# Linear attention block: v's weight applied once per sequence to x^T k, instead of v per tile

## The chip, the cores and the metric

The kernel runs on one core of a Trainium2 chip. The metric is the device time of one execution in microseconds, 2818.39 us as the median of three runs (2816.66 to 2820.75). Engines are called by the names of the profile: PE is TensorE, with PEld its weight loads; DVE is VectorE, ACT is ScalarE, POOL is GpSimd, and SP the engine that issues most of the DMAs.

## The reference, cut to what matters

The input is 16 sequences of 1024 tokens with 512 channels, float32. The block is a linear attention with 16 heads of 32 channels, and then a channel mix; each is added to its input and followed by a layer norm.

```python
qkv = x @ Wqkv.T + bqkv
q, k, v = jnp.split(qkv, 3, axis=-1)
q = rmsnorm(q, gq)
k = rmsnorm(k, gk)
q, k, v = (split(q), split(k), split(v))
q = apply_rope(q, cos, sin)
k = apply_rope(k, cos, sin)
qf = jax.nn.relu(q)
kf = jax.nn.relu(k)
vpad = jnp.concatenate([v, jnp.ones_like(v[..., :1])], axis=-1)
vk = jnp.einsum('bhlp,bhld->bhpd', vpad, kf)
res = jnp.einsum('bhpd,bhld->bhlp', vk, qf)
attn = res[..., :-1] / (res[..., -1:] + EPS_LIN)
attn = attn.transpose(0, 2, 1, 3).reshape(B, L, D)
out = rmsnorm(attn @ Wout.T + bout, gout)
...
x = _layernorm(x + attention(x))
x = _layernorm(x + channel_mix(x))
```

Only vk needs v: per head it is the sum over the sequence's tokens of v times k, and the sum of the keys. Since v = x Wv^T + bv, the sum of v k^T is Wv (sum of x k^T) plus bv times the sum of the keys.

## The kernel before

Tokens are handled in 128 tiles of 128, eight to a sequence. Every float32 product is made of three products of a faster type: hi hi + hi lo + lo hi, where hi is the operand rounded by a copy on ACT and lo the rest, by a subtraction mostly on DVE.

**Part one** (lines 226 to 519) runs `slot(i)` for every tile and three more. A slot loads x of tile i + 2 with channels first (`load_xt`) and the table of tile i + 1 (`tables`: the RMS norm's weight times the rope's cosine and sine; made on POOL for the first eight tiles, L337, stored, and loaded again from then on). On PE it projects q and k (`proj`, L312: 12 matmuls of 512 columns each), then v (12 more), then adds the previous tile's k^T v to four PSUM banks that stand for the whole sequence (`add_kv`, L399 and L407: for each group of four heads a matmul of 258 columns with k's hi and one of 130 with its lo; the columns are v's hi, the keys' scale as hi and lo, and v's lo). On DVE and ACT it adds the bias of q and k (L353), takes the squares (L354), from which POOL takes a power -0.5 (`rsqrt`, L115), multiplies by the two tables (L364, L365), combines them to the rope (L367, L368), splits relu(k) (L373, L374) and scales v (L385, L386, L388, L389); x of the next tile is split (L247, L248). q goes to DRAM through SP (L370). Beside it, `late_weight` splits one chunk of the later weights per slot, the low part on POOL (L258).

At the end of each sequence `finish_a` (one slot after the last add_kv) reads the four banks, masks what doesn't belong to one head, stores the keys' sums and adds v's bias; `finish_b`, a slot later, transposes and splits; `finish_c` multiplies by the output weight in four further slots (L454) and stores the result `m_d`.

Seven tiles (NPRE = 7) begin their second part beside part one, one every eight slots from slot 40 on; the first four go all the way through `part_y` there, the others through `part_q`.

**Part two** (from line 521) takes q, divides by its product with the keys' sums (`part_q`), multiplies by the sequence's matrix (`part_qt`, `part_m`), normalizes (`part_y`), and then runs the channel mix by halves of a sequence (`part_t`, `part_fk`, `part_fr`, `part_fv`), all of whose products are L130. Its pools open as part one's close: `wb` (mixed tokens for the gate, squared keys) right after part one's tiles, `wr` with the gate's weight after slot N has ended the pool of k and v.

The order of the instructions on each engine, SP's DMAs too, is made by the planner of the tile framework from its own estimates of when each becomes ready; each engine then takes its list in order.

Of the kernel before, what the change touches and what calls it, by code (L numbers as in the profile page):

```python
# [17 lines left out]
NC_ = DIM // P  # chunks of 128 channels  # L18
# [3 lines left out]
VW = 2 * P + 2  # v's hi of four heads, the keys' scale as hi and lo, v's lo  # L22
NPRE = 7  # tiles whose second part begins beside the first part
FIRST, STEP = 40, 8  # the first of them, and how many tiles of the first part lie between two
XA = 7  # x tiles in the pool of both parts
XB = 4  # and in the second part's own
HT = 512  # tokens in a half of a sequence
NT = HT // P  # tiles of 128 tokens in a half
# [6 lines left out]
def kernel(  # L35
# [19 lines left out]
    """Post-norm block: relu linear attention with rope, then an RWKV channel mix.  # L55

    x and out are [tiles, 128, 512]; xt is x by tiles with channels first, [tiles, 128, 4, 128]
    (channel = 128 * third + second). Weights are [128, 4, out] with the input channel split the
    same way. Within a head the channels of q and k come even ones first. The rope tables are
    [128, 8, 16] (position = 128 * second + first).  # L60

    A float32 product is three float32r products: hi hi + hi lo + lo hi, with x = hi + lo.
    """
    nc = tc.nc
    V, S, G, T = nc.vector, nc.scalar, nc.gpsimd, nc.tensor
    N = x.shape[0]  # tiles
    NB = N // 8  # sequences
    NH = N // NT  # halves
# [14 lines left out]
    # The second part's own pools, once they are open: x, the sequences' matrices, banks.  # L83
    own = {}

    def ring(tag, n, outer, inner, shape, dtype, name):
        """Slot n of a ring that lies in the pool of both parts and in the second part's own."""
        k = n % (outer + inner)
        pool, size = (wp, outer) if k < outer else (own[tag], inner)
        return pool.tile(shape, dtype, tag=tag, bufs=size, name=name)  # L90
# [17 lines left out]
    # The activation table comes in before the data does.  # L108
# [16 lines left out]
    def product(ps, pairs, rows, cols):  # L125
        """ps = sum over chunks of a^T b, with a and b given as (hi, lo)."""
        n = len(pairs)
        for c, (a, b) in enumerate(pairs):
            for k, (u, w) in enumerate(((0, 0), (0, 1), (1, 0))):
                T.matmul(  # L130
                    ps,
                    lhsT=a[u][:, rows],
                    rhs=b[w][:, cols],
                    start=(c == 0 and k == 0),
                    stop=(c == n - 1 and k == 2),
                )

# [24 lines left out]
    def part_q(j):  # L162
        """relu(q) over its product with the keys' sums."""
# [36 lines left out]
    def layernorm(xt, sm, name):  # L200
        """(x - mean) / sqrt(var + eps), in place; sm holds the sums."""
# [10 lines left out]
    def part_y(j, ps):  # L212
        """Output's bias, its RMS norm, the residual and the layer norm: x becomes x1."""
# [12 lines left out]
    # ================= part one: q, k, v and each sequence's k^T v =================  # L226
    with ExitStack() as a_ctx:
        # What outlives the last tile's projections lies on the other side.
        te = a_ctx.enter_context(tc.tile_pool(name="end", bufs=1, side="right"))
        pa_ctx = a_ctx.enter_context(ExitStack())  # L230
        tk_ctx = a_ctx.enter_context(ExitStack())
        tk = tk_ctx.enter_context(tc.tile_pool(name="endkv", bufs=1, side="right"))
# [18 lines left out]
        w_qkv = {h: ca.tile([P, NC_, 3 * DIM], F32R, name=f"wqkv_{h}") for h in "hl"}  # L251
# [10 lines left out]
        for j in range(3):  # L262
            cols = slice(j * DIM, (j + 1) * DIM)
            for c in range(NC_):
                n = NC_ * j + c
                split_w(
                    w_qkv["h"][:, c, cols],
                    w_qkv["l"][:, c, cols],
# [3 lines left out]
                    *(("x", XA), ("q", 3), ("y", 2))[(n >= XA) + (n >= XA + 3)],  # L272
# [13 lines left out]
        for n, m in (("k", mu_k), ("r", mu_r)):  # L286
# [4 lines left out]
        bvm = te.tile([P, NC_, P], F32, name="bvm")  # L291
        nc.scalar.dma_start(
            out=bvm.rearrange("p g n -> p (g n)"),
            in_=bqkv[2 * DIM : 3 * DIM].partition_broadcast(P),
        )
        # Ones where row and column belong to one head of a group of four.
        mask = te.tile([P, P], F32, name="mask")
# [3 lines left out]
        for g in range(NC_):  # L301
            V.tensor_mul(bvm[:, g, :], bvm[:, g, :], mask)
        state = {}
        ps_kv = {}

        def proj(i, j):
            """A third of the tile's q, k, v."""
            ps = bank(f"ps{'qkv'[j]}{i}")
            cols = slice(j * DIM, (j + 1) * DIM)
            for c in range(NC_):  # L310
                for n, (a, b) in enumerate(((xh, "h"), (xh, "l"), (xl, "h"))):
# [3 lines left out]
                        rhs=w_qkv[b][:, c, cols],  # L315
# [13 lines left out]
        def tables(i):  # L329
            """RMS norm's weight times the rope's cosine and sine, for the positions of tile i."""  # L330
            tab[i] = wa.tile([P, 2, 2 * DIM], F32, tag="tab", bufs=2, name=f"tab{i}")
            t = i % 8
            if i >= 8:
                nc.sync.dma_start(out=tab[i], in_=tab_d[t])
                return
            for n, tb in enumerate((cos, sin)):
                (V if i == 0 and n else G).tensor_mul(  # L337
                    rows(tab[i][:, n, :]),
                    rows(g_qk),
                    tb[:, t, :].unsqueeze(1).to_broadcast([P, 4 * HEADS, HH]),  # L340
                )
            tab_d[t] = dram.tile([P, 2, 2 * DIM], F32, name=f"tab_d{t}")
            nc.sync.dma_start(out=tab_d[t], in_=tab[i])
# [3 lines left out]
        def norm(i, ps):  # L347
            """Bias, and RMS norm's scale (kept apart)."""
            qk = wa.tile([P, 2 * DIM], F32, tag="qk", bufs=2, name=f"qk{i}")
# [8 lines left out]

        def rope(i):
            """RMS norm's weight and the rope; the keys' relu."""  # L360
            qk, tb = qks.pop(i), tab.pop(i)
            t1 = wa.tile([P, 2 * DIM], F32, tag="t1", bufs=1, name=f"t1{i}")
            ro = wa.tile([P, 2 * DIM], F32, tag="ro", bufs=2, name=f"ro{i}")
            V.tensor_mul(t1, qk, tb[:, 0, :])  # L364
            V.tensor_mul(qk, qk, tb[:, 1, :])  # L365
            a1, a2, o = halves(t1), halves(qk), halves(ro)
            V.tensor_sub(o[:, :, 0, :], a1[:, :, 0, :], a2[:, :, 1, :])  # L367
            V.tensor_add(o[:, :, 1, :], a2[:, :, 0, :], a1[:, :, 1, :])  # L368
            q_d[i] = dram.tile([P, DIM], F32, name=f"q_d{i}")
            nc.sync.dma_start(out=q_d[i], in_=ro[:, 0:DIM])  # L370
            kh = tk.tile([P, DIM], F32R, tag="kh", bufs=2, name=f"kh{i}")
            kl = tk.tile([P, DIM], F32R, tag="kl", bufs=2, name=f"kl{i}")
            S.activation(kh, ro[:, DIM : 2 * DIM], AF.Relu)  # L373
            V.scalar_tensor_tensor(  # L374
                kl, ro[:, DIM : 2 * DIM], 0.0, f32(kh), ALU.max, ALU.subtract
            )
            return kh, kl

        def scale_v(i, ps):
            """v times the keys' scale, and the scale itself."""  # L380
            v = tk.tile([P, NC_, VW], F32R, tag="v", bufs=2, name=f"v{i}")
            rs = rstd_all[:, i, 1:2]
            pv = groups(ps)
            vh, vl = v[:, :, 0:P], v[:, :, P + 2 : VW]
            S.activation(vh, pv, AF.Copy, scale=rs)  # L385
            V.scalar_tensor_tensor(vl, pv, rs, f32(vh), ALU.mult, ALU.subtract)  # L386
            rb = rs.unsqueeze(1).to_broadcast([P, NC_, 1])
            V.tensor_copy(v[:, :, P : P + 1], rb)  # L388
            V.tensor_sub(v[:, :, P + 1 : P + 2], rb, f32(v[:, :, P : P + 1]))  # L389
            return v  # L390

        def add_kv(i):
            kh, kl, v = state.pop(i)
            b, t = i // 8, i % 8
            if t == 0:
                ps_kv[b] = pa.tile([P, NC_, DIM], F32, tag="kv", bufs=1, name=f"pskv{b}")
            for g in range(NC_):
                cols = slice(g * P, (g + 1) * P)
                T.matmul(  # L399
                    ps_kv[b][:, g, 0:VW],  # L400
                    lhsT=kh[:, cols],
                    rhs=v[:, g, :],
                    start=(t == 0),
                    stop=False,
                    skip_group_check=True,
                )
                T.matmul(  # L407
                    ps_kv[b][:, g, 0 : P + 2],
                    lhsT=kl[:, cols],
                    rhs=v[:, g, 0 : P + 2],  # L410
                    start=False,
                    stop=(t == 7),
                    skip_group_check=True,
                )

        fin = {}

        def finish_a(b):
            """Block diagonal k^T v (with v's bias) by groups of four heads; the keys' sums."""
            ps = ps_kv.pop(b)  # L420
            kc = te.tile([P, NC_], F32, tag="kc", name=f"kc{b}")
            V.reduce_sum(kc, ps[:, :, P : P + 2], AX.X)
            kv = te.tile([P, NC_, P], F32, tag="kv", name=f"kv{b}")
            S.copy(kv, ps[:, :, P + 2 : VW])
            V.tensor_add(kv, kv, ps[:, :, 0:P])
# [352 lines left out]
```

## Time and profile before

| what | value |
|---|---|
| median of three runs | 2818.39 us |
| profiled execution, span | 2818.5 us |
| instructions | 39315 |
| granted PE clock, mean over the span | 0.994 |
| a tile's DVE work in part one | L364 1.22, L365 1.23, L353 twice 0.69, L248, L367, L368, L374 0.69 each, L386 0.74 us |
| a tile's ACT work in part one | L354 twice 0.63, L247 0.62, L373 0.63, L385 0.69 us |
| POOL in part one, from tile 8 on | L115, 1.65 us a tile |
| loads of a table (1 MB) | 120, 5.2 us from issue to landing |

The profile names a group of instructions by its line, engine and operation, with what it writes and reads. A duration on PE is from issue to the modelled end, and matmuls overlap: how often a new one starts is what counts. The clock of PE granted in the first 100 us is below one, and full after that. DVE's and POOL's durations contain what an instruction waited for inside itself, after it was issued.

### The profile page before, as it was taken

The page shows a single profiled execution, that of the slowest core. Times are in us where ns is not written, and L with a number is a line of the kernel's source. Part 1 is how long each engine was busy: PE and PEld are TensorE (multiplying, and loading weights), DVE is VectorE, ACT ScalarE, POOL GpSimd, SP SyncE. Part 2 cuts the span into 40 slices and gives each one's busy share as a digit, 9 for nine tenths or more (in the row PEclk, how much of TensorE's full clock was granted, in tenths as well). Part 3 has the DMA queues.
Part 4 walks back from the last instruction along what each step waited for, and adds up shares of the span by engine and source line. Part 5 has one row for each costly group of instructions (what it writes and reads, how often), then busy time and mean ns, then how long its engine had stood idle before and what let it go on. Part 6 is the DMA issues. An engine that isn't in the chain of part 4 may idle for free.

```text
span 2818.5 us, 39315 instructions
## 1 busy us (share of the span) xinstructions
PE 2769.1 (98%) x13072; PEld 2295.8 (81%) x13072; DVE 2278.0 (81%) x4999; ACT 1608.8 (57%) x3199; POOL 859.8 (31%) x823
## 2 busy tenths in 40 slices
PE   7899999999999999998999999999999999999998
PEld 5788888888888888887788888888888888888887
DVE  7998888888888888887878788877888787878774
ACT  3343334444333333435677767777777777777775
POOL 7431111111111111113433333333333333333331
PEclk9999999999999999999999999999999999999999
DMA  7566666665656556556132313231323132323210
GB/s 248 190 240 207 189 209 202 192 191 188 202 197 194 207 197 199 187 178 218 64 106 92 111 61 109 87 116 57 113 85 107 64 112 87 101 72 100 81 53 34
DMA packets 165146, 397.78 MB, mean 141 GB/s; under 512 B 24272, under 2 KB 24528, under 8 KB 148560
## 3 DMA queue, kind: packets, MB, share of 16 engines
q1 hardware_dynamic: 162784, 391.74, 42.7%
q10 hardware_dynamic: 2160, 3.54, 0.4%
q8 instruction: 103, 1.69, 0.2%
q14 instruction: 99, 0.81, 0.1%
HBM read 279.84 MB, written 115.38 MB: 140 GB/s over the span
## 4 chain that ended last, share of the span: by engine, by line
PE 50%; DVE 1%; issue 0%; ACT 0%; POOLq 0%; POOL 0%; ACTq 0%
PE psv L130 12%; PE psk L130 12%; PE psr L130 12%; PE psy L130 11%; PE pst L538 2%; PE psqt L181 2%; DVE gate L653 0%; DVE mrl L559 0%; DVE x L655 0%; ACT x L210 0%; DVE mixr L548 0%; DVE pr L166 0%; DVE mixk L548 0%; DVE nmf L209 0%; ACT junkf L205 0%
## 5 line engine op out<-in xcount | busy, mean ns | idle before, releaser
L115 POOL TENSOR_TENSOR rstd_all<-ss,mhalf 128x2 f32<-128x2 f32 x128 | 208.8, 1631 | 911.9 <-DVE ss L355 911.7
L354 ACT ACTIVATE junk<-qk 128x512 bf16<-128x512 f32 x256 | 161.6, 631 | 387.2 <-DVE qk L353 386.4
L130 PE MATMUL psk<-mkh,w_k 128*128 128x512 f32 x1024 | 333.0, 397 | 0.0
L130 PE MATMUL psv<-w_v,kah 128*128 128x512 f32 x1024 | 326.5, 400 | 0.0
L130 PE MATMUL psr<-w_r,mrh 128*128 128x512 f32 x1024 | 323.2, 397 | 0.0
L130 PE MATMUL psy<-mb,qth 128*128 128x512 f32 x1024 | 319.5, 393 | 2.0 <-ACT qth L184 2.0
L221 POOL TENSOR_TENSOR y<-y,g_out 128x512 f32<-128x512 f32 x128 | 168.9, 1319 | 327.8 <-ACT junky L217 326.1
L559 POOL TENSOR_TENSOR mkl<-mixk,mkh 128x512 fp32r<-128x512 f32 x128 | 175.6, 1373 | 182.8 <-ACT mkh L558 182.8
L130 PEld LDWEIGHTS psy<-mb,qth 128*128 128x128 f32 x1024 | 191.8, 188 | 44.7 <-ACT qth L184 2.3
L130 PEld LDWEIGHTS psk<-mkh,w_k 128*128 128x128 f32 x1024 | 193.1, 189 | 39.2
L130 PEld LDWEIGHTS psv<-w_v,kah 128*128 128x128 f32 x1024 | 188.1, 188 | 40.4
L130 PEld LDWEIGHTS psr<-w_r,mrh 128*128 128x128 f32 x1024 | 188.3, 189 | 36.5
L312 PE MATMUL psq<-wqkv_h,xh 128*128 128x512 f32 x512 | 205.4, 401 | 11.6 <-ACT wqkv_h L257 6.4
L312 PE MATMUL psq<-wqkv_l,xh 128*128 128x512 f32 x512 | 203.7, 398 | 0.2 <-POOL wqkv_l L258 0.2
L312 PE MATMUL psq<-wqkv_h,xl 128*128 128x512 f32 x512 | 202.8, 396 | 0.8 <-DVE xl L248 0.8
L130 PE MATMUL psv<-w_v,kal 128*128 128x512 f32 x512 | 202.1, 395 | 0.0
L312 PE MATMUL psv<-wqkv_h,xh 128*128 128x512 f32 x512 | 200.3, 391 | 1.7 <-DVE qk L353 1.2
L312 PE MATMUL psk<-wqkv_h,xh 128*128 128x512 f32 x512 | 200.0, 391 | 2.0 <-DVE v L386 1.8
L130 PE MATMUL psy<-mb,qtl 128*128 128x512 f32 x512 | 201.5, 393 | 0.0
L312 PE MATMUL psv<-wqkv_l,xh 128*128 128x512 f32 x512 | 200.3, 391 | 0.9 <-POOL wqkv_l L258 0.9
L130 PE MATMUL psr<-w_r,mrl 128*128 128x512 f32 x512 | 200.9, 392 | 0.0
L312 PE MATMUL psv<-wqkv_h,xl 128*128 128x512 f32 x512 | 200.8, 392 | 0.0
(135 smaller groups left out, 7252.4 us busy)
## 6 DMA issues: line engine op xcount, KB each, us to landing
tab<-tab_d SPq DMA_DIRECT2D x120, 1024.0 KB, 5.2
xt<-in_xt_dram SPq DMA_DIRECT2D x128, 256.0 KB, 4.8
q_d<-ro SPq DMA_DIRECT2D x128, 256.0 KB, 4.6
m_d<-m SPq DMA_DIRECT2D x64, 512.0 KB, 4.1
mb<-m_d SPq DMA_DIRECT2D x64, 512.0 KB, 7.0
q<-q_d SPq DMA_DIRECT2D x128, 256.0 KB, 2.6
x<-in_x_dram SPq DMA_DIRECT2D x128, 256.0 KB, 2.8
out_dram<-x SPq DMA_DIRECT2D x128, 256.0 KB, 3.0
```

The lines of the kernel that those rows point to most:

```text
L115: G.tensor_tensor(dst, src, mhalf[:, 0 : src.shape[1]], ALU.pow)
L130: T.matmul(ps, lhsT=a[u][:, rows], rhs=b[w][:, cols], start=(c == 0 and k == 0), stop=(c == n - 1 and k == 2),)
L181: T.transpose(ps[:, c, :], q[:, c * P : (c + 1) * P], ident)
L221: G.tensor_mul(y, y, g_out)
L312: T.matmul(ps, lhsT=a[i][:, c, :], rhs=w_qkv[b][:, c, cols], start=(c == 0 and n == 0), stop=(c == NC_ - 1 and n == 2),)
L354: S.activation(junk(f"{i}{j}"), qk[:, cols], AF.Square, accum_out=ss[:, j : j + 1])
L538: T.transpose(ps[:, t * P : (t + 1) * P], xs[NT * s + t][:, c * P : (c + 1) * P], ident)
L559: (V if n == "r" and s != 1 else G).tensor_sub(ml, m, f32(mh))
```

## The change

v is not computed per tile any more. The tile's x is loaded a second time with tokens first, split into hi and lo (`split_xn`: hi on ACT, lo on POOL), and `add_kx` accumulates x^T k over the sequence in four PSUM banks: 12 matmuls of 512 columns per tile. ACT multiplies k by its scale in the relu, and the keys of a sequence are added up on POOL in `acc`. Once per sequence, `finish_a` takes x^T k out of PSUM as hi and lo, `finish_s` sums `acc` over the tokens with a matmul by ones, and `finish_b` multiplies by v's weight (`w_a`), adds v's bias times the keys' sums, masks on POOL and splits. `finish_c` is as it was. v's weight leaves the weights split ahead of the first tile and comes first among the late ones.

The table is now two tiles with one buffer each instead of one with two, `qk` has one buffer instead of two, the rope's first product is written into `ro`, NPRE is 6 instead of 7, and the x tiles are 6 + 5 instead of 7 + 4. `tables(i + 1)` stands at the end of a slot instead of its beginning; `finish_c` stands ahead of `add_kx`. At the handover, slots N + 1 and N + 2 come ahead of the pools `wb` and `wr` and of the load of the gate's weight.

```diff
-NPRE = 7  # tiles whose second part begins beside the first part
+NPRE = 6
-XA = 7  # x tiles in the pool of both parts
-XB = 4  # and in the second part's own
+XA = 6
+XB = 5
...
+        def split_xn(i):
+            w = wa.tile([P, DIM], F32, tag="xn", bufs=1, name=f"xn{i}")
+            nc.sync.dma_start(out=w, in_=x[i])
+            h = tk.tile([P, DIM], F32R, tag="xnh", bufs=2, name=f"xnh{i}")
+            l = tk.tile([P, DIM], F32R, tag="xnl", bufs=2, name=f"xnl{i}")
+            S.copy(h, w)
+            G.tensor_sub(l, w, f32(h))
+            xn[i] = h, l
...
-        for j in range(3):
+        for j in range(2):
...
-        for g in range(NC_):
-            V.tensor_mul(bvm[:, g, :], bvm[:, g, :], mask)
...
+            tab[i] = [
+                wa.tile([P, 2 * DIM], F32, tag=f"tab{n}", bufs=1, name=f"tab{n}{i}")
+                for n in range(2)
+            ]
...
-            qk = wa.tile([P, 2 * DIM], F32, tag="qk", bufs=2, name=f"qk{i}")
+            qk = wa.tile([P, 2 * DIM], F32, tag="qk", bufs=1, name=f"qk{i}")
...
         def rope(i):
-            V.tensor_mul(t1, qk, tb[:, 0, :])
-            V.tensor_mul(qk, qk, tb[:, 1, :])
-            a1, a2, o = halves(t1), halves(qk), halves(ro)
-            V.tensor_sub(o[:, :, 0, :], a1[:, :, 0, :], a2[:, :, 1, :])
-            V.tensor_add(o[:, :, 1, :], a2[:, :, 0, :], a1[:, :, 1, :])
+            V.tensor_mul(ro, qk, tb[0])
+            V.tensor_mul(qk, qk, tb[1])
+            a2, o = halves(qk), halves(ro)
+            V.tensor_sub(o[:, :, 0, :], o[:, :, 0, :], a2[:, :, 1, :])
+            V.tensor_add(o[:, :, 1, :], a2[:, :, 0, :], o[:, :, 1, :])
...
-            S.activation(kh, ro[:, DIM : 2 * DIM], AF.Relu)
-            V.scalar_tensor_tensor(
-                kl, ro[:, DIM : 2 * DIM], 0.0, f32(kh), ALU.max, ALU.subtract
-            )
-            return kh, kl
+            S.activation(k, k, AF.Relu, scale=rstd_all[:, i, 1:2])
+            S.copy(kh, k)
+            V.tensor_sub(kl, k, f32(kh))
+            b, t = divmod(i, 8)
+            ros[i] = k
+            if t == 1:
+                acc[b] = tx.tile([P, DIM], F32, tag="acc", name=f"acc{b}")
+                G.tensor_add(acc[b], ros[i - 1], k)
+            if t > 1:
+                G.tensor_add(acc[b], acc[b], k)
+            return kh, kl
...
+        def add_kx(i):
+            kh, kl = state.pop(i)
+            h, l = xn.pop(i)
...
+            for c in range(NC_):
+                cols = slice(c * P, (c + 1) * P)
+                for n, (a, r) in enumerate(((h, kh), (h, kl), (l, kh))):
+                    T.matmul(
+                        ps_kx[b][c],
+                        lhsT=a[:, cols],
+                        rhs=r,
+                        start=(t == 0 and n == 0),
+                        stop=(t == 7 and n == 2),
+                    )
...
+        def finish_a(b):
+            kx = tx.tile([P, NC_, NC_, 2, P], F32R, tag="kx", name=f"kx{b}")
+            for c, ps in enumerate(ps_kx.pop(b)):
+                S.copy(kx[:, c, :, 0, :], groups(ps))
+                V.tensor_sub(kx[:, c, :, 1, :], groups(ps), f32(kx[:, c, :, 0, :]))
+            fin[b] = kx
+
+        def finish_s(b):
+            a = acc.pop(b)
+            m = te.tile([P, 2, DIM], F32R, tag="m", bufs=2, name=f"ma{b}")
+            S.copy(m[:, 0, :], a)
+            G.tensor_sub(m[:, 1, :], a, f32(m[:, 0, :]))
+            ps = bank(f"psks{b}")
+            for n in range(2):
+                T.matmul(ps, lhsT=ones, rhs=m[:, n, :], start=(n == 0), stop=(n == 1))
+            ksv[b] = tx.tile([P, DIM], F32, tag="ksv", name=f"ksv{b}")
+            S.copy(ksv[b], ps)
...
+        def finish_b(b):
+            kx, ks = fin.pop(b), ksv.pop(b)
...
+            for g in range(NC_):
+                cols = slice(g * P, (g + 1) * P)
+                ps = bank(f"pskv{b}{g}")
+                for c in range(NC_):
+                    T.matmul(
+                        ps[:, 0 : 2 * P],
+                        lhsT=w_a["h"][:, c, cols],
+                        rhs=kx[:, c, g, :, :].rearrange("p two n -> p (two n)"),
...
+                    T.matmul(
+                        ps[:, 0:P],
+                        lhsT=w_a["l"][:, c, cols],
+                        rhs=kx[:, c, g, 0, :],
...
+                kv = te.tile([P, P], F32, tag="kv", bufs=1, name=f"kv{b}{g}")
+                V.scalar_tensor_tensor(
+                    kv, ks[:, cols], bv[:, g : g + 1], ps[:, 0:P], ALU.mult, ALU.add
+                )
+                V.tensor_add(kv, kv, ps[:, P : 2 * P])
+                G.tensor_mul(kv, kv, mask)
+                S.copy(th[:, g, :], kv)
+                G.tensor_sub(tl[:, g, :], kv, f32(th[:, g, :]))
...
-        late = [("o", wout, c) for c in range(NC_)]
+        late = [("a", wqkv[:, :, 2 * DIM : 3 * DIM], c) for c in range(NC_)]
+        late += [("o", wout, c) for c in range(NC_)]
...
         tk_ctx.close()
+        slot(N + 1)
+        slot(N + 2)
+        tx_ctx.close()
+        wb = ctx.enter_context(tc.tile_pool(name="workb", reuse_waits="tile", bufs=1))
         wr = ctx.enter_context(tc.tile_pool(name="workr", reuse_waits="tile", bufs=1))
         load_w("r", wr)
-        slot(N + 1)
         pa_ctx.close()
-        slot(N + 2)
```

## The prediction

> **What bounds the kernel now.** I read the page's busy table and its forty slices first, then the windows by stage, then the groups of lines inside one undisturbed sequence, and last the timeline of the first tiles.
>
> The page, busy time and slices:
>
> ```profile
> PE 2769.1 (98%) x13072; PEld 2295.8 (81%) x13072; DVE 2278.0 (81%) x4999; ACT 1608.8 (57%) x3199; POOL 859.8 (31%) x823
> ...
> PE   7899999999999999998999999999999999999998
> PEld 5788888888888888887788888888888888888887
> DVE  7998888888888888887878788877888787878774
> ACT  3343334444333333435677767777777777777775
> POOL 7431111111111111113433333333333333333331
> ```
>
> TensorE is full except at the start and in slices 18 and 19, where part one hands over. VectorE is next, eight tenths full. GpSimd is busy in the first two slices, nearly empty through part one, and busier again in part two.
>
> Windows (length, then busy time of each engine, granted clock, DMA share, GB/s):
>
> ```profile
> 46.50:112.30 65.80, 56.48 (x234) 45.65 (x234) 63.99 (x73) 19.96 (x42) 44.92 (x20) 0.88 0.63 228
> 112.30:1270.80 1158.50, 1157.09 (x5585) 973.09 (x5584) 960.78 (x1695) 461.94 (x961) 215.00 (x138) 1.00 0.61 198
> 1270.80:1450.00 179.20, 166.00 (x779) 135.36 (x778) 146.99 (x342) 120.58 (x236) 78.33 (x81) 0.97 0.42 135
> ...
> 332.00:408.30 76.30, 76.30 (x370) 64.22 (x369) 62.31 (x109) 30.01 (x62) 13.20 (x8) 1.00 0.60 193
> ```
>
> The first is six slots (tiles 1 to 7): VectorE is full (63.99 of 65.80), TensorE is not. The second is slots 7 to 127, where TensorE has no gap. The third is the handover, 13.2 us of TensorE idle. The last is one sequence, eight slots: 76.3 us, TensorE 76.3, VectorE 62.3, ScalarE 30.0, GpSimd 13.2. So in steady state TensorE sets the time and VectorE has 14 us of slack per sequence.
>
> Groups inside that sequence:
>
> ```profile
> L399 PE MATMUL pskv<-v,kh 128*128 128x258 f32 x32 | 7.9, 319 | 0.0
> L407 PE MATMUL pskv<-v,kl 128*128 128x130 f32 x32 | 7.3, 227 | 0.0
> L440 PE MATMUL pskvt<-ident,kv 128*128 128x128 f32 x4 | 0.6, 272 | 0.0
> L353 DVE TENSOR_TENSOR qk<-psk,b_qk 128x512 f32<-128x512 f32 x8 | 5.5, 692 | 9.7 <-PE psk L312 9.6
> L386 DVE SCALAR_TENSOR_TENSOR v<-psv,rstd_all,v 128x512 fp32r<-128x512 f32 x8 | 6.0, 744 | 0.0
> ```
>
> The matmul rows overlap, so I price TensorE from start to start in the timeline: twelve psv matmuls run from 802.36 to 805.09, 0.227 each; the eight of add_kv from 805.09 to 805.97, 0.88 a slot, 0.22 for a pair of 258 and 130 columns.
>
> The first tiles, VectorE and then GpSimd (start, duration):
>
> ```profile
> 96.24 0.68 DVE L367 TENSOR_TENSOR ro<-t,qk 128x512 f32<-128x512 f32 x1
> 96.84 2.88 DVE L368 TENSOR_TENSOR ro<-qk,t 128x512 f32<-128x512 f32 x1
> 99.65 2.30 DVE L388 CAST v<-rstd_all 128x4 fp32r<-128x4 f32 x1
> 101.99 0.17 DVE L389 TENSOR_TENSOR v<-rstd_all,v 128x4 fp32r<-128x4 f32 x1
> 102.07 0.68 DVE L353 TENSOR_TENSOR qk<-psq,b_qk 128x512 f32<-128x512 f32 x1
> ```
>
> ```profile
> 96.23 2.94 POOL L337 TENSOR_TENSOR tab<-g_qk,cos 128x1024 f32<-128x1024 f32 x1
> 99.14 2.78 POOL L337 TENSOR_TENSOR tab<-g_qk,sin 128x1024 f32<-128x1024 f32 x1
> ```
>
> L368 takes 0.685 in the steady state; here it ends half a microsecond after the GpSimd multiply beside it (99.17). The cast after it waits out the next multiply. VectorE and GpSimd take turns. Operations with a PSUM input are spared: L353 and L386 keep 0.68 and 0.74 in this window. That is the view that decides this case.
>
> **TensorE.** Per slot v's twelve matmuls go and twelve of x^T k come, both 512 wide: 12 x 0.227 each way, nothing. add_kv goes: 8 x 0.88 = 7.0 a sequence, and four transposes, 4 x 0.11 = 0.4. Added per sequence: two 512-wide matmuls for the keys' sum, 0.45, and 16 pairs of 256 and 128 columns at 0.22, 3.5. Net 7.4 - 4.0 = 3.5 us a sequence, so 76.3 becomes 72.8. Over the fifteen sequences of the second window: -52 if TensorE stays the bound.
>
> **VectorE.** Per sequence, out: L386 8 x 0.744, and L388 and L389 8 x (0.172 + 0.162), together 8.6; finish_a and finish_b lose a reduce 0.16, an add 0.68, a multiply 0.69, four L431 at 0.347 and one L444 0.68, 3.6. In: four subtractions from PSUM at 0.685, 2.7; four L431-like and four 128-wide adds, the latter between 0.16 (L389) and 0.347, I take 0.28: 2.5. Splitting the keys stays one operation of 0.68. 62.3 - 8.6 - 3.6 + 2.7 + 2.5 = 55.4.
>
> **GpSimd.** Alone, a two-input 128x512 operation takes 1.29 (L221 in part one), a power 0.55 (two or one columns, from the rows with none of VectorE's work beside them; the 1.65 of L115 is mostly a wait for L365). Per sequence: eight xnl 10.3, seven sums of keys 9.0, one split of the sum 1.3, eight powers 4.4, and eight 128-wide operations of finish_b between 0.55 and 1.29, I take 0.55: 4.4. Together 29.4, against 13.2 busy now.
>
> **What that costs VectorE.** In the 65.8 us window its instructions' durations add up to 69.5; at their undisturbed durations they would be 47.6. So 21.9 were lost. GpSimd's work there, at its undisturbed lengths, is ten table multiplies at 2.37, four splits at 1.29 and six powers at 0.55: 32.2. The ratio is 0.68: each microsecond of GpSimd took 0.68 from a full VectorE. Bounds for the new mix: 0 if every GpSimd operation falls into VectorE's idle time or beside an operation that reads PSUM, 1 if none does. I take 0.68: 0.68 x 29.4 = 20.0, and VectorE needs 55.4 + 20.0 = 75.4 a sequence. That is more than TensorE's 72.8: **VectorE, blocked by GpSimd, becomes the bound, about where TensorE was.**
>
> [...]
>
> The tiles of part two that begin in part one now cost VectorE instead of TensorE: six part_q at 2.76 (L166 to L173), four times part_qt and part_y at some 2.6 plus 1.6 of blocking: 33.5 in all. Steady state: 15 x 75.4 + 33.5 = 1164.5 against 1158.5, **+6**. One hundredth of the ratio is 4.4 us, so break-even for the whole kernel is near 0.64.
>
> **The first tiles.** Six slots at 10.97. VectorE loses 1.08 a slot; GpSimd gains an xnl and a sum, 2.58, and is charged 0.68 of it, 1.75, plus more of the weight splits, which are one a slot for twenty slots instead of sixteen: I take +1.6 a slot, +10, and 4 x 1.29 x 0.68 = 3.5 for the four chunks of v's weight that now come late. Ahead of them: four fewer weight chunks before the first slot, and the four multiplications of v's bias by the mask are gone (7.34 us from 38.62 on, each blocked). I take -6, between -10 and 0. Sum **+7**.
>
> **The handover.** finish_b of the last sequence has 3.5 us more of matmuls and, with one buffer for kv, four rounds VectorE, GpSimd, ScalarE, GpSimd of 0.35 + 0.28 + 0.55 + 0.35 + 0.55 = 2.1 us instead of one wait of 1.83. The pool of part two's gate mix and squared keys now opens only after it, and so do four 512 KB loads of the gate's weight (13.5 us to land). Cover: three early tiles, transposes, four key products of 2.7 us that need only banks. If that cover is short, up to 20; I take **+6**, from -3 to +20.
>
> **At nothing.** x is read once more, 256 KB a slot on SP: DMA share 0.60, by bytes about 0.69. ScalarE rises from 30 to some 37 of 76. A table half is now loaded into its only buffer: freed at the end of its multiply, it lands 5.2 us later and is needed a slot of 9.4 us less 1.2 after that. Its cover is 1.6 to 3 us; see the last rival. Part two's steady state is untouched.
>
> **Sum.** 2818.5 (the profiled span; the median of the runs is 2818.4, the same) + 6 + 7 + 6 = 2837.5, say **2838**.
>
> **Rivals.** (1) TensorE stays the bound: the GpSimd operations fall beside q's and k's bias additions (16 a sequence, spared) and into VectorE's 9.7 us of waits for psk. For it: 17 us of room a sequence below 72.8, and a ratio under 0.59 is enough. Against it: the room is only there as long as VectorE is not late. 2818.5 - 52 + 7 + 6 = **2779**. (2) kv's single buffer stops VectorE: between two groups of finish_b it waits for a GpSimd multiply, a ScalarE copy and a GpSimd subtraction, 1.45 us, four times in sixteen sequences: +93, **2931**. It decides once VectorE has no slack and the order puts nothing between the groups; behind the waiting instruction stand q's and k's bias additions, and behind them the banks. The order is made by a planner that I can't see, hence half of it is as likely: 2885. (3) The tables come late, with q's store ahead of them on SP: 1.8 us in 120 slots, about 3030.
>
> **Chances.** Forecast (2815 to 2870): 0.42. TensorE bound: 0.33. kv's buffer, whole or in part: 0.21. Tables: 0.04. Less than 0.2% (5.6 us, what this kernel's measurement can't tell from nothing) takes 0.08, most of it from the forecast's lower end. Faster 0.34, same 0.08, slower 0.58. The forecast's own range is 2815 to 2870; for 8 in 10, 2774 to 2912.
>
> **What would show it.** After: VectorE 9 in the slices of part one and TensorE below, waits of TensorE there on VectorE; L367-, L368-like and key-split rows well over 0.69, the bias additions not; GpSimd near 30 us a sequence or more; about 75 to 76 us from sequence to sequence. If TensorE has no gap in part one and a sequence takes 73, the first rival holds; if VectorE idles on GpSimd or ScalarE in finish_b, the second. I am wrong altogether if the bias additions are blocked as well, or nothing is.

## The result, and the profile after

The changed kernel takes 2853.59 us (median of four runs, 2852.93 to 2854.51) against 2817.52 before: a ratio of 1.0125, 95% interval 1.0111 to 1.0139. It is 36 us slower; 20 were forecast. The profiled execution spans 2851.2 us, 32.7 more than before.

The page after, busy time and slices:

```profile
PE 2753.0 (97%) x12528; PEld 2251.1 (79%) x12528; DVE 2309.2 (81%) x4674; ACT 1698.0 (60%) x3455; POOL 1288.0 (45%) x1209
...
PE   6899998999999999998999999999999999999998
PEld 5677876777887878886788888888888888888887
DVE  8888888888888888887787878787878787878774
...
POOL 8765544554555555554533333333333333333341
PEclk9899999999999999998999999999999999999999
```

TensorE has 16 us less busy time and a longer span. Between tiles 7 and 127 GpSimd has gone from 19% to 52% of the time. VectorE is not at 9 there, as I had said it would be; it went from 83% to 84%.

The windows after (length, busy time of each engine, granted clock, DMA share, GB/s): the first tiles, tiles 7 to 127, the handover, then a sequence that carries a tile's second part, and a quiet one:

```profile
46.50:108.00 61.50, 50.14 (x186) 38.91 (x185) 58.74 (x47) 19.30 (x44) 57.94 (x28) 0.86 0.45 167
108.00:1293.00 1185.00, 1138.23 (x5064) 927.48 (x5063) 997.04 (x1388) 545.13 (x1205) 618.76 (x506) 0.98 0.69 224
1293.00:1480.00 187.00, 171.16 (x781) 138.59 (x780) 145.18 (x342) 124.23 (x241) 83.46 (x90) 0.94 0.39 132
...
423.00:513.10 90.10, 81.03 (x349) 64.90 (x348) 72.65 (x107) 38.05 (x84) 39.99 (x35) 0.94 0.67 226
1143.20:1218.80 75.60, 74.02 (x331) 61.02 (x330) 64.30 (x89) 35.31 (x78) 38.74 (x32) 0.98 0.68 222
```

Between tiles 7 and 127, TensorE now idles 47 us (1.4 before), and its granted clock is 0.98 instead of 1.00. The quiet sequence takes 75.6 us, 0.2 from my number, but VectorE is busy for 64.3 of them and not for all.

From the start of the first table multiplication of tiles 7, 39, 71 and 127, the time falls into five stages. Sequences are counted from tile 7, eight tiles each; the first two carry late weights, the fifth to eighth a tile's second part each; the last column is from tile 127's multiplication to the end of the span.

| us | to tile 7 | seq. 1 to 4 | 5 to 8 | 9 to 15 | to the end |
|---|---|---|---|---|---|
| before | 112.3 | 304.9 | 322.1 | 531.6 | 1547.7 |
| after | 108.0 | 315.0 | 342.0 | 527.8 | 1558.3 |
| change | -4.3 | +10.1 | +19.9 | -3.8 | +10.6 |
| e1, no wide GpSimd work | 104.6 | 297.6 | 319.1 | 509.8 | 1556.9 |
| e2, it is on VectorE | 108.9 | 303.5 | 317.1 | 512.3 | 1556.1 |
| e3, four kv | 108.3 | 310.9 | 345.0 | 514.4 | 1552.3 |
| e4, scale on x | 109.7 | 309.8 | 333.1 | 519.9 | 1557.3 |
| e5, e2 and e3 | 108.7 | 302.0 | 314.6 | 510.9 | 1555.6 |
| e9, and late weights spread | 109.0 | 299.4 | 312.1 | 510.8 | 1551.8 |

So the loss is 30 us in the first eight sequences, in six of which GpSimd and VectorE have something more to do (called loaded below), and 11 in the handover; the seven quiet ones gain only 4, where TensorE's saved work, 3.2 us each (76.3 before against the 73.1 that e1 and e3 reach below), would give 22.

VectorE's groups in the quiet sequence (busy, mean ns, then idle time before them and what ended it):

```profile
L384 DVE TENSOR_TENSOR ro<-qk,tab 128x1024 f32<-128x1024 f32 x8 | 12.6, 1573 | 0.1
L396 DVE TENSOR_TENSOR kl<-ro,kh 128x512 fp32r<-128x512 f32 x8 | 8.2, 1024 | 9.0 <-ACT kh L395 9.0
L249 DVE TENSOR_TENSOR xl<-xt,xh 128x512 fp32r<-128x512 f32 x9 | 7.7, 853 | 0.0
L388 DVE TENSOR_TENSOR ro<-qk,ro 128x512 f32<-128x512 f32 x8 | 6.6, 822 | 0.0
L372 DVE TENSOR_TENSOR qk<-psq,b_qk 128x512 f32<-128x512 f32 x8 | 5.5, 689 | 0.6
L372 DVE TENSOR_TENSOR qk<-psk,b_qk 128x512 f32<-128x512 f32 x8 | 5.5, 684 | 0.0
L477 DVE SCALAR_TENSOR_TENSOR kv<-ksv,bv,pskv 128x128 f32<-128x128 f32 x4 | 1.4, 340 | 1.3 <-POOL kvtl L483 1.3
```

Four operations with two inputs in SBUF are drawn out beside GpSimd: the first multiplication from 1.22 to 1.57, the split of the keys from 0.68 to 1.02, that of x from 0.69 to 0.85, the last step of the rope from 0.69 to 0.82; together 8 us. The bias additions, which read PSUM, are not (0.69 and 0.68). And there is an idle time that I hadn't priced: 9.0 us in which VectorE stands before the split of the keys until ScalarE has made their high half. For TensorE it doesn't wait in this sequence.

What TensorE waits for in that sequence shows in the timeline at finish_b, TensorE and then VectorE (start, duration, wait in brackets):

```profile
1165.32 0.33 PE L460 MATMUL pskv<-kx,wa_h 128*128 128x256 f32 x1
...
1165.55 0.34 PE L460 MATMUL pskv<-kx,wa_h 128*128 128x256 f32 x1
1165.72 0.22 PE L468 MATMUL pskv<-kx,wa_l 128*128 128x128 f32 x1
1167.34 0.39 PE L460 MATMUL pskv<-kx,wa_h 128*128 128x256 f32 x1 [1.39 <-DVE qk L372]
...
1169.27 0.52 PE L460 MATMUL pskv<-kx,wa_h 128*128 128x256 f32 x1
1169.59 0.31 PE L468 MATMUL pskv<-kx,wa_l 128*128 128x128 f32 x1
1169.69 0.52 PE L460 MATMUL pskv<-kx,wa_h 128*128 128x256 f32 x1
```

```profile
1166.60 0.68 DVE L372 TENSOR_TENSOR qk<-psq,b_qk 128x512 f32<-128x512 f32 x1
1167.20 0.68 DVE L372 TENSOR_TENSOR qk<-psk,b_qk 128x512 f32<-128x512 f32 x1
```

finish_b asks for four banks of a ring of four. The next of them still holds q's projection, which VectorE reads only at 1166.60. TensorE stands for 1.39 us. Less than a microsecond after the gap, at 1168.18, the granted clock falls to half, for 3.41 us: a pair of matmuls takes 0.42 (1169.27 to 1169.69) instead of 0.23 (1165.32 to 1165.55). But that isn't what makes a quiet sequence longer than 73.1 us: sequences 11 to 13, with a wait of 1.1 to 1.4 us at the same place and a granted clock of 1.00 throughout, take 75.6 or 75.7 us as well.

### The profile page after: what moved, and what is told of

The parts are those of the page before. It is cut to its first block, busy times and chain, and to the rows that moved or that the text cites. A ratio compares the mean times of both kernels' runs of the same rounds, so it can differ in the third digit from the quotient of the medians.

```text
span 2851.2 us, 39461 instructions
## 1 busy us (share of the span) xinstructions
PE 2753.0 (97%) x12528; PEld 2251.1 (79%) x12528; DVE 2309.2 (81%) x4674; ACT 1698.0 (60%) x3455; POOL 1288.0 (45%) x1209
## 4 chain that ended last, share of the span: by engine, by line
PE 52%; DVE 1%; ACT 1%; issue 0%; POOL 0%; POOLq 0%; ACTq 0%
PE psk L129 12%; PE psr L129 12%; PE psv L129 12%; PE psy L129 12%; PE psqt L180 2%; PE pst L579 2%; DVE x L222 0%; DVE pr L165 0%; PE pskx L419 0%; DVE mixr L593 0%; DVE mixr L589 0%; DVE y L214 0%; ACT junka L204 0%; ACT x L209 0%; PE psm L493 0%
## 5 line engine op out<-in xcount | busy, mean ns | idle before, releaser
L392 ACT ACTIVATE ro<-ro,rstd_all 128x512 f32<-128x512 f32 x128 | 92.7, 724 | 430.2 <-POOL rstd_all L114 270.2
L327 PE MATMUL psq<-wqk_h,xh 128*128 128x512 f32 x512 | 207.3, 405 | 30.9 <-DVE qk L372 12.4
L261 POOL TENSOR_TENSOR xnl<-xn,xnh 128x512 fp32r<-128x512 f32 x128 | 183.7, 1435 | 96.3 <-ACT xnh L260 93.2
L396 DVE TENSOR_TENSOR kl<-ro,kh 128x512 fp32r<-128x512 f32 x128 | 130.3, 1018 | 106.5 <-ACT kh L395 106.5
L419 PE MATMUL pskx<-kl,xnh 128*128 128x512 f32 x512 | 208.2, 407 | 6.1 <-DVE kl L396 6.1
L419 PE MATMUL pskx<-kh,xnl 128*128 128x512 f32 x512 | 206.8, 404 | 0.0
L327 PE MATMUL psq<-wqk_h,xl 128*128 128x512 f32 x512 | 205.6, 401 | 0.8 <-DVE xl L249 0.8
L327 PE MATMUL psq<-wqk_l,xh 128*128 128x512 f32 x512 | 205.6, 402 | 0.0
L327 PE MATMUL psk<-wqk_h,xh 128*128 128x512 f32 x512 | 201.6, 394 | 3.5 <-DVE qk L372 1.7
L114 POOL TENSOR_TENSOR rsa<-sqa,mhalf 128x1 f32<-128x1 f32 x128 | 81.0, 633 | 268.1 <-DVE sqa L205 200.8
```

The costliest lines, as they stand in the source:

```text
L114: G.tensor_tensor(dst, src, mhalf[:, 0 : src.shape[1]], ALU.pow)
L261: G.tensor_sub(l, w, f32(h))
L327: T.matmul(ps, lhsT=a[i][:, c, :], rhs=w_qk[b][:, c, cols], start=(c == 0 and n == 0), stop=(c == NC_ - 1 and n == 2),)
L392: S.activation(k, k, AF.Relu, scale=rstd_all[:, i, 1:2])
L396: V.tensor_sub(kl, k, f32(kh))
L419: T.matmul(ps_kx[b][c], lhsT=a[:, cols], rhs=r, start=(t == 0 and n == 0), stop=(t == 7 and n == 2),)
```

## The experiments

All are changes of the changed kernel unless said otherwise, and all ratios are to the kernel before, whose median was 2817 to 2818 us beside them.

**e1: no wide GpSimd work.**

```diff
+            if i == 0:
+                xn_l.append(tk.tile([P, DIM], F32R, tag="xnl", bufs=1, name="xnl"))
+                G.tensor_sub(xn_l[0], w, f32(h))
+            xn[i] = h, xn_l[0]
...
-            if t > 1:
-                G.tensor_add(acc[b], acc[b], k)
```

> Leaves out two things: the low half of x is made for tile 0 alone and used for every tile, and only the first two tiles of a sequence are added up in the keys' sum; so GpSimd loses 14 of its 16 wide operations per sequence (18 us) and no other engine gets work. Theory A (GpSimd's wide operations block VectorE, and that is where the time goes): the sequences in part one fall from 75.6 us to TensorE's 72.8, those with late weights and with second parts from 80 to 90 by about as much again, and the whole to 2775 to 2795. Rival B (one buffer for qk, for a table and for kv, and the chain power, scaled relu, copy, split of the keys): those stay as they are, the sequences stay at 75 and the whole above 2835.

2788.34 us, ratio 0.9893 (0.9873 to 0.9913). The quiet sequences take 73.1 us and TensorE is without a gap in them; sequences 1 to 4 lose 17 us, 5 to 8 lose 23. As theory A had it. The handover stays (1556.9), so GpSimd's work per tile has no part in that. The run takes away the work; it doesn't tell whether the drawing out of VectorE's instructions beside GpSimd's (8 us in the changed kernel's quiet sequence) or the lateness of what GpSimd delivers is the cause.

**e2: the same work on VectorE.**

```diff
-            G.tensor_sub(l, w, f32(h))
+            V.tensor_sub(l, w, f32(h))
...
-                G.tensor_add(acc[b], acc[b], k)
+                V.tensor_add(acc[b], acc[b], k)
```

> The low half of x and the sum of the keys are made on VectorE instead of GpSimd. Theory A: VectorE gets 16 x 0.69 = 11 us a sequence of its own and loses the waits of 20.6 us of GpSimd work; at the ratio of 0.31 that the changed kernel shows in its quiet sequences this is a loss of 4 us a sequence, at my 0.68 a gain of 3; so 2830 to 2880, with the first sequences, where GpSimd is full of tables and weights, gaining most. Rival B: VectorE waits for the keys anyway, 9 us a sequence, so the 11 us are half hidden: 2855 to 2900.

2800.66 us, ratio 0.9938 (0.9923 to 0.9953): faster than before, and outside both expectations on the good side. Windows of a sequence with a second part and of a quiet one:

```profile
412.40:497.90 85.50, 81.30 (x360) 66.36 (x359) 74.20 (x123) 39.72 (x86) 19.49 (x20) 0.96 0.73 243
1096.30:1169.40 73.10, 73.10 (x336) 60.36 (x335) 67.52 (x104) 35.83 (x79) 19.27 (x17) 1.00 0.71 230
```

VectorE does 15 more wide operations in the quiet sequence, some 10 us, and is busy for only 3.2 us more than in the kernel with them on GpSimd (67.5 against 64.3). There GpSimd had cost it some 8 us of drawn out instructions, and 9 of waits for the keys stood beside them (1.2 here). Its first multiplication is at 1.25 us again in the loaded sequence (1.46 there with GpSimd).

**e3: four kv.** kv of all four groups lies in one buffer of the ring m.

```diff
+            kvs = te.tile([P, 2 * NC_, P], F32, tag="m", bufs=2, name=f"kvs{b}")
...
-                kv = te.tile([P, P], F32, tag="kv", bufs=1, name=f"kv{b}{g}")
+                kv = kvs[:, g, :]
```

> kv of all four groups lies in one buffer of the m ring instead of one group after the other in a single buffer. Rival B, in the form of my second rival: VectorE no longer waits for GpSimd in finish_b (1.3 us a sequence in the quiet ones) and TensorE no longer for the banks (1.7 us a sequence): 2815 to 2835. Theory A: the waits were in slack, and the result is within 6 us of 2851.

2829.24 us, ratio 1.0033 (1.0019 to 1.0047); 24 us under the changed kernel, as the rival had it. Its windows, a loaded and a quiet sequence:

```profile
419.20:509.10 89.90, 82.72 (x367) 66.69 (x366) 73.33 (x108) 38.07 (x84) 40.73 (x35) 0.96 0.68 226
1132.70:1205.80 73.10, 73.10 (x336) 60.42 (x335) 61.03 (x89) 36.38 (x79) 41.05 (x32) 1.00 0.72 230
```

With GpSimd as busy as after (41.05 us), the quiet sequence is down to 73.1 and TensorE has no gap; no bank is missing at finish_b. The planner's order changed there too, so the run doesn't tell the buffer itself from the order that it allows. The loaded one stays at 90. And the handover loses 6 us. So there are two losses: one at the end of each sequence, which either e2 or e3 takes away, and one in the loaded sequences, which e2 takes away and e3 doesn't.

**e4: the keys' scale on x.**

```diff
-            S.copy(h, w)
-            G.tensor_sub(l, w, f32(h))
+            rs = rstd_all[:, i, 1:2]
+            S.activation(h, w, AF.Copy, scale=rs)
+            V.scalar_tensor_tensor(l, w, rs, f32(h), ALU.mult, ALU.subtract)
...
-            S.copy(kh, k)
-            V.tensor_sub(kl, k, f32(kh))
+            S.activation(kh, k, AF.Relu)
+            V.scalar_tensor_tensor(kl, k, 0.0, f32(kh), ALU.max, ALU.subtract)
+            S.activation(k, k, AF.Relu, scale=rstd_all[:, i, 1:2])
```

> The keys' scale goes to x with tokens first (a scaled copy on ScalarE, the low half on VectorE with the scale) instead of the keys, whose high half is then one relu straight from the rope; the scaled relu for the keys' sum follows off the path. VectorE's split of the keys waits for one ScalarE operation instead of two and no longer for the power. Theory A: it loses 8 GpSimd operations a sequence as e2 does in part, with 5.5 us more on VectorE: 2835 to 2860. Rival B (the chain is what holds VectorE, 9 us a sequence): VectorE's waits for the keys fall below 3 us a sequence, sequences reach 73, and the whole is 2800 to 2825.

2830.84 us, ratio 1.0044 (1.0029 to 1.0059). VectorE's waits for the keys' high half fall from 99.3 us in part one to 5.6, as rival B had it; but the quiet sequences are at 74.1, not 73, and the time lies between the two expectations, 4 us under theory A's and 6 over rival B's. The run takes half of the wide work off GpSimd as well and can't tell which of the two gave its 23 us; e10, beside e5, tries the chain alone.

**e5 and e6: with four kv, both on VectorE, or x's low half alone.** e5 is e2 and e3; e6 leaves the keys' sum on GpSimd.

> e2 and e3 together: the low half of x and the keys' sum on VectorE, and four buffers for kv. Theory A2 (two separate losses: kv's single buffer at the end of each sequence and at the handover, and GpSimd's wide operations where VectorE is full, in the sequences with tables, late weights and second parts): the sequences keep e2's times, and the handover falls by e3's 4 to 6 us: 2787 to 2797. If VectorE, at 70 of 73 us, is now the bound itself, kv's buffer doesn't matter or the order gets worse: 2798 to 2815.

> As e5, but only the low half of x goes to VectorE; the keys' sum stays on GpSimd. Theory A2: half of GpSimd's wide work stays, so the loaded sequences lie between e3's and e2's and the quiet ones at 73.1: 2800 to 2815. If it is the number of VectorE's own operations that costs in the loaded sequences, this beats e5: below 2790.

e5: 2793.0 us, ratio 0.9912 (0.9898 to 0.9925). e6: 2804.13 us, ratio 0.9948 (0.9935 to 0.9962). Both times are as theory A2 says, but not all of its parts: e5's handover is 1555.6, as e2's 1556.1, and not 4 to 6 us less; what e5 gains over e2 lies in the sequences. Beside e5, e6's seven GpSimd additions a sequence cost 11 us, 10 of them in sequences 5 to 8 (324.5 against 314.6).

**e7 and e8: GpSimd work put into the kernel before.** e8 is the kernel before with NPRE 6 and x tiles 6 + 5, e7 has two GpSimd subtractions per tile on top, whose result nobody reads.

```diff
+            for _ in range(2 if i < N else 0):
+                G.tensor_sub(
+                    extra,
+                    xh[i].rearrange("p c n -> p (c n)").bitcast(F32),
+                    xl[i].rearrange("p c n -> p (c n)").bitcast(F32),
+                )
```

> The kernel before with NPRE 6 and x tiles 6 + 5, and two GpSimd subtractions of 128x512 per tile (x's high and low half, of which nothing is used): 20.6 us of GpSimd work a sequence and nothing else. By my ratio 0.68 VectorE is blocked for 14 us a sequence, just its slack of 14: quiet sequences stay at 76.3 to 78, the first tiles take 1.8 us a tile more, those with second parts some 5 us a sequence more; 2840 to 2875. By the ratio 0.31 of the changed kernel the quiet sequences stay at 76.3 exactly and the whole is 2825 to 2845. If GpSimd's work doesn't matter, as e8.

> The kernel before with NPRE 6 and x tiles 6 + 5 alone, the control of e7: one tile less begins in part one, which moves some 3 us of work behind it and takes little cover from the handover: 2812 to 2826.

e8: 2824.32 us, ratio 1.0027 (1.0018 to 1.0037). e7: 2949.52 us, ratio 1.047 (1.0456 to 1.0484): 125 us for 256 unused GpSimd operations, more than twice what I expected at most. A quiet sequence takes 82.6 instead of 76.3. VectorE's groups in one of them, and GpSimd's:

```profile
L369 DVE TENSOR_TENSOR ro<-qk,t 128x512 f32<-128x512 f32 x8 | 14.3, 1782 | 0.0
L390 DVE TENSOR_TENSOR v<-rstd_all,v 128x4 fp32r<-128x4 f32 x8 | 9.3, 1165 | 0.0
L387 DVE SCALAR_TENSOR_TENSOR v<-psv,rstd_all,v 128x512 fp32r<-128x512 f32 x8 | 5.9, 739 | 0.0
L389 DVE CAST v<-rstd_all 128x4 fp32r<-128x4 f32 x8 | 1.4, 171 | 4.1 <-POOL rstd_all L115 4.1
```

```profile
L490 POOL TENSOR_TENSOR extra<-xh,xl 128x512 f32<-128x512 f32 x16 | 25.9, 1621 | 7.7 <-DVE xl L248 6.9 <-DVE v L389 0.2
```

One operation of 0.69 takes 1.78 and a tiny one of 0.16 takes 1.17, each behind one of the two subtractions; L387, which reads PSUM and comes as the second ends, stays at 0.74. That is 8 x (1.10 + 1.00) = 16.8 us of VectorE for 16 x 1.29 = 20.6 us of GpSimd, a ratio of 0.81. VectorE is full (78.3 busy and 4.1 of wait for the power, of 82.6), and TensorE, 79.2 busy, waits for it. Nothing reads what these subtractions make, and the wait for the power is 4.1 in a sequence of the kernel before as well; so this shows by itself what VectorE loses beside GpSimd.

**e9: late weights spread.** e5, with part two's weights split one every third tile after tile 8.

```diff
-            if 1 <= i and late and i < N:
+            if 1 <= i and late and i < N and (i <= 8 or i % 3 == 0):
```

> e5 with the twelve weights of part two split one every third tile from tile 9 on, instead of one per tile up to tile 20. Theory A2: what the first two sequences lose over the quiet ones (80.6 and 76.7 against 73.2 in e5, 11 us) comes from these GpSimd splits beside a full VectorE and from their loads; spread over slack they cost little, but the first seven tiles' share, and the tables', stays: 4 to 8 us less than e5, 2785 to 2789. If the first sequences are slow from the tables and from TensorE's half clock after each gap alone: as e5, 2791 to 2795.

2784.53 us, ratio 0.9884 (0.9868 to 0.9901), 8.5 under e5: 2.6 in sequences 1 to 4, where the expectation had put all of it, 2.5 in 5 to 8, 3.8 in the handover. This version is 33 us faster than before and 69 faster than the changed kernel. Its quiet sequence:

```profile
1085.10:1158.30 73.20, 73.20 (x336) 60.40 (x335) 67.34 (x105) 35.56 (x79) 18.26 (x17) 1.00 0.70 230
```

Why the handover gained, the run doesn't tell: the planner's order changed there too.

**e10: e5 with the scale on x.**

> e5 with the keys' scale on x as in e4: the same operations, but the keys' split waits for one ScalarE operation and not for the power. Theory A2: in the quiet sequences TensorE is the bound already (73.2) and nothing is gained there; in the loaded ones VectorE's waits for the keys (19 us in part one) go: 2783 to 2793. If the waits only move to the low half of x, which now needs the power: 2793 to 2805.

2792.38 us, ratio 0.9913 (0.9898 to 0.9927): the same as e5, at the far edge of theory A2's expectation. Once GpSimd's wide work is on VectorE, the chain of the keys has no part in the time that shows.

**e11 and e12: the second buffer of qk.** It needs 4 KB, so both have NPRE 4 and x tiles 4 + 7.

```diff
-            qk = wa.tile([P, 2 * DIM], F32, tag="qk", bufs=1, name=f"qk{i}")
+            qk = wa.tile([P, 2 * DIM], F32, tag="qk", bufs=2, name=f"qk{i}")
```

> The changed kernel with NPRE 4 and x tiles 4 + 7 (two tiles' divisions move from part one behind it): the control of e12, whose second buffer needs that room. Theory A2: two divisions less beside a full VectorE, but less cover in the handover: 2845 to 2860.

> e11 with two buffers for qk, as before the change. Rival B (the single buffer of qk holds VectorE back): at least 10 us under e11. Theory A2: within 6 us of e11.

e11: 2858.9 us, ratio 1.0151 (1.0134 to 1.0168). e12: 2856.2 us, ratio 1.014 (1.0124 to 1.0155). The second buffer gives nothing that can be told. Second buffers for the tables were not tried.

## Why the prediction was right, and where it wasn't

The direction held, and so did the reason, GpSimd's wide work against VectorE. The sum was 19 us where the profile shows 33, and its parts were off on both sides: +6 forecast between tiles 7 and 127 and +26.5 measured, +7 and -4.3 ahead of them, +6 and +10.6 behind.

**TensorE's work.** I had 72.8 us a sequence; e1, e2 and e3 show 73.1, with no gap. Right.

**The ratio of 0.68.** It was measured on a full VectorE and taken for a constant. Where VectorE is full, e7 measures 0.81. In the quiet sequences of the changed kernel it isn't full: 64.3 busy less my 55.4 of its own work is 8.9 of GpSimd's 29.4, 0.30. The ratio is no constant; that it follows VectorE's own slack fits both numbers, but no run varies the slack alone. Nor does a run show why an instruction of one engine stands while the other's runs; shown is how long.

**VectorE the bound of the quiet sequences.** That is the step that failed, though its 75.4 us is 0.2 from what was measured; that is luck. VectorE is busy for 64.3 us, not 75.4: what it loses beside GpSimd is 8.9 where I had 20.0, and some 10 us are waits for ScalarE and GpSimd (9.0 for the keys, 1.3 at kv) where I had none. The two errors cancel. Nor is that loss the bound by itself: e3 leaves GpSimd's work as it is, and TensorE is full, at 73.1. My second rival had the place, the single buffer of kv, but the wrong price: 5.8 us a sequence of VectorE's waits, where VectorE waits 1.3 and TensorE stands 1.1 to 1.4 for a bank. I gave it 0.21; it is worth 24 us in e3, on top of the first mechanism and not in its place.

**The loaded sequences.** The second parts were to cost 33.5 us, 28 of them in sequences 5 to 8, and cost 39.6 there over four quiet sequences (342.0 - 4 x 75.6). The four more chunks of late weights were priced at 3.5 us and counted to the first tiles; sequences 1 and 2 take 83.3 and 79.9, 12 us over two quiet ones. Both were too small. With the wide work on VectorE (e2) the second parts cost 24.7 over four of its quiet sequences, so GpSimd's part in that term is shown. Its sequences 1 and 2 still cost 11.1 over two quiet ones; without the wide work on either engine (e1) they cost 5.1. What the rest of that term is made of stays open.

**The first tiles.** +7 forecast, -4.3 measured. Tile 1's multiplication starts 9.8 us earlier (36.8 against 46.6; I had taken 6), and a tile then takes 11.9 us instead of 11.0, +0.9 where I had +1.6 and the late weights' 3.5 on top.

**The handover.** +6 forecast, +10.6 measured. Four buffers for kv take 6 off it in e3, but next to nothing in e5 (1555.6 against e2's 1556.1). Beginning one tile less in part one costs e8 6 us here, from 1547.7 to 1553.9, which I hadn't priced at all; but beginning two tiles less still doesn't cost e11 anything here (1554.8 against 1558.3). All the versions with the change lie between 1551.8 and 1562.2, and which cause makes how much of it stays open; the later pools were not tried alone.

**What was to cost nothing.** x's second load and ScalarE's work cost the quiet sequences nothing: e1, e2 and e3 have both, and TensorE is full in them. The tables' single buffers cost little: in part one VectorE waits for a table 5.3 us once, in the fifth sequence, and 4.4 us in two other places. The third rival is out.

Settled is that GpSimd's wide operations cost the loaded sequences (e5 takes 39 us off e3's sequences 1 to 8), that where VectorE is full they draw out its own instructions, by 0.81 us for each microsecond of GpSimd's in e7, and that kv's buffer, or the order it forces, costs the ends of the sequences. Not settled is how much of the rest is TensorE's half clock, 49.8 us in stretches that begin in or just behind a gap, as no run holds the clock apart from the gaps.

## What to carry to other kernels

An engine's share of busy time in the profile isn't room for another engine's work: price elementwise work moved to GpSimd at what it takes from VectorE, here 0.81 of its length where VectorE was full (e7) and 0.30 in the changed kernel's quiet sequences, and try it on VectorE first. Here 15 operations a sequence are cheaper on the engine that looked nearly full than on the one that looked empty. When a stage takes as many banks of a ring at once as the ring has, look who still holds the first of them: here that was 1.39 us of TensorE.

## What the runs showed of the hardware

**TensorE's half clock began in its gaps or just behind them.** Between the start of tile 7's first table multiplication and the handover, the trace's record of the clock has no stretch at half speed before the change and ten after, 3.41 or 6.83 us long each (the first of them begins 1.4 us ahead), 49.8 us together. Each begins during a wait of TensorE or less than a microsecond behind one. A matmul pair of 0.23 us takes 0.42 in the one shown. At half speed 49.8 us are worth at most 24.9 of TensorE's work. With the 47 us that it idles that makes 72, close to the 26.5 us lost and the 48 (15 times 3.2) of its work that the change saves. In e9, with 10.5 us of TensorE idle there, the mean granted clock is 1.00, against 0.98. The clock is not full to the end before the change either: its handover has three stretches of 3.41 us.

Not each gap has one: the stretches at 789.3 and 1168.2 came behind waits of 1.5 and 1.4 us, and a wait of 1.66 us, up to 209.11, had none behind it. What decides, these runs don't show.

**What VectorE lost beside GpSimd didn't follow the size of its operation.** In e7 a VectorE operation of 4 columns waits 1.0 us behind a GpSimd operation of 512, as long as one of 512 columns does (1.10).
